# A four-layer macaron kernel on one core: five re-orderings, from the second layer's weight preparation to the first unit of the last attention

## The chip, the core and the metric

The kernel runs on one core of one Trainium2 chip. The metric is the device time of one execution in microseconds (us). The core has a matrix engine (TensorE, PE), a vector engine (VectorE, DVE), a scalar engine (ScalarE, ACT), a general engine (GpSimd, POOL) and a queue engine that issues most DMAs (SyncE, SP). Each works through its own instructions in their program order and waits on semaphores of the others. All data are fp32.

## The reference

Four batches of 512 tokens of width 128 run through four layers. Each layer adds half of a feed-forward block, then an attention (or scan), then half of the same feed-forward block again:

```python
x = x + 0.5 * L0_ffn(layernorm(x)); x = x + L0_attn(layernorm(x)); x = x + 0.5 * L0_ffn(layernorm(x))
x = x + 0.5 * L1_ffn(layernorm(x)); x = x + L1_attn(layernorm(x)); x = x + 0.5 * L1_ffn(layernorm(x))
x = x + 0.5 * L2_ffn(layernorm(x)); x = x + L2_attn(layernorm(x)); x = x + 0.5 * L2_ffn(layernorm(x))
x = x + 0.5 * L3_ffn(layernorm(x)); x = x + L3_attn(layernorm(x)); x = x + 0.5 * L3_ffn(layernorm(x))
```

- L0_ffn: top-1 mixture of 8 experts (128 to 512 to 128, relu) with a capacity of 320 tokens per expert. L3_ffn: top-2 mixture of 8 experts with capacity 512. Tokens beyond an expert's capacity are dropped.
- L1_ffn: sigmoid gate, top 2 of 8 small swiglu experts plus a shared one. L2_ffn: top 2 of 8 linear experts, `gates[e] * ((x @ w_in[e].T) @ w_out[e].T)`, so that each expert is one 128x128 matrix, m = w_out·w_in.
- L0_attn and L1_attn: causal softmax attention with 16 heads of 8 (the former with a table of relative positions, the latter with the product of two low-rank scores). L2_attn: gated decaying scan. L3_attn: full (not causal) softmax attention of 16 heads of 8 over 512 keys, with a layernorm of its own, x + out.

## The kernel before

A batch b is a tile `xs[b]` of 128 partitions by NT = 4 tiles by 128. Feed-forward blocks of layers 1 and 2 are run by pairs of batches, `pairs = [[0, 1], [2, 3]]`. A stage is written as a Python generator; `skewed(gens, lag)` (L1519) advances several of them in turn, the i-th beginning i * lag rounds later, and so writes the order in which each engine's instructions stand. `whole` runs one generator to its end. Outside of `manual_schedule` a planner may move instructions a little; inside, the order written is the order of the queues.

**Mixtures (layers 0 and 3).** `tokens` (L296) normalises a batch's rows (`norms`, L168–L186: BN_STATS and BN_AGGR per tile on DVE, rs and rstd on POOL, then n on ACT or DVE), transposes them (T_f, L195), makes logits (L330), masks (L344 and what follows), the rank of a token within its expert (rank_f, three matmuls at L373 and after) and its target row (`to`, L405–L409), and scatters the rows into a buffer in DRAM, `disp`, with indirect DMAs that POOL issues (L416). The top-2 mixture has two copies of the buffer, one per choice. `experts` (L426) then loads the rows of an expert (d, and d2 for the second copy), and `prepare` (L452) joins them: where a row lies behind the first choice's rows (`behind`, 0 or 1), d2's row is added to d (L457 a multiplication of 128x520, L458 an addition of 128x512, L459 an addition of the two trailing columns). Then four transposes (dT, L463), a copy on ACT (L465), two matmul stages (h_f L487, o_f L523) and a scatter back (L509). `combine` (L533) loads a batch's results (r, L538) and adds them to x (L539). The mixture objects in order are f00 and f01 (layer 0, before and after attention) and f30, f31 (layer 3).

**Layer 2's weights.** `prep_l2` (L1296) loads w_in and w_out of the 8 experts during f01's experts, and then for each expert e transposes w_out (wo2T, L1326), copies it out of PSUM, makes m_e with four matmuls of 2 passes (L1331), and copies that. The copies go through `copy` (L131–L136), which alternates between DVE (L134) and ACT (L136): here all copies of wo2T are DVE's and all of m ACT's.

**Layer 1's first feed-forward block** follows. The main body first runs `f01.combine(b)` for all four batches, then `skewed([followed(pool, bs) for bs in pairs], 12)`; `followed` is `l1_ffn` (L1134: normalise, transpose T_f, logits, routing chain mx L226 to comb L1089, transposed gates gT L1127, expert matmuls), and for pair 0 also the beginning of layer 1's attention.

**Layer 3's dispatch.** At the end of the chain of layers 1 and 2 (`behind` in the main body), the last pair's two batches go through `f30.tokens` with `skewed(..., 3)`.

**Attention 3** is the helper `attention` (L597) without an additive table. A unit u is a batch b and a group g of 4 heads, 16 units in all. For each unit it works in two passes over the scores: `largest` multiplies queries by keys (s_a, L618) and takes each query's negated largest score with DVE (low, L707, 128x512); `lowered` (L709–L716) transposes low and adds it to the queries (ql); `by_key` makes the scores again, keys by (lowered) queries (t_a, L618), whose exponential on ACT (L727) is the weight w, already transposed; `times_values` (L750) multiplies w with the values (L757). `step(f, n)` is one half of one tile (two of the four heads); `together` takes two steps and sets their products in turn. `lead = 10` steps of `largest` are run ahead, with `lowered(0)` after eight (16 reduces); then the loop over u from 0 pairs the largest of 10 steps ahead with the weights of now. Between them stand `start(u + 2)` (q and k of a later unit), `normalized` (L773) and, through `begin_next`, the parts of the next batch's `begin` (L1456: combine's adds, BN, n2 and n, T, qk, values). Each of the four heads lies in its own 32 rows (SLOT) of the array. Products of a query or key tile go to one PSUM bank of 512 columns each; there are 8 banks.

Of the kernel before, what the change touches and what calls it, by code (L numbers as in the profile page):

```python
# [17 lines left out]
P = 128  # L18
# [23 lines left out]
def kernel(ctx: ExitStack, tc: tile.TileContext, a: dict, out: bass.AP):  # L42
# [170 lines left out]
    def bc(ap, shape):  # L213
        while len(ap.shape) < len(shape):
            ap = ap.unsqueeze(len(ap.shape))
        return ap.to_broadcast(shape)
# [28 lines left out]
    class Mixture:  # L245
# [180 lines left out]
        def experts(self, w, beside=None):  # L426
# [3 lines left out]
            with tc.tile_pool(name=f"moe_{self.tag}", bufs=2) as pool:  # L430
# [21 lines left out]
                def prepare(e):  # L452
                    tag = f"{e}_{self.tag}"
                    d = got[e, 0]
                    if self.k == 2:
                        d2 = got[e, 1]
                        nc.vector.tensor_tensor(d2, d2, bc(behind[:, e, :], [P, per, W]), ALU.mult)  # L457
                        nc.vector.tensor_tensor(d[:, :, :D], d[:, :, :D], d2[:, :, 2:], ALU.add)  # L458
                        nc.vector.tensor_tensor(d[:, :, D:], d[:, :, D:], d2[:, :, :2], ALU.add)  # L459
                    ps = bank(f"dT{tag}")  # L460
                    for s in range(per):
                        m = min(P, cap - s * P)
                        nc.tensor.transpose(ps[:, s * P : s * P + m], d[:m, s, :D], ident[:m, :m])  # L463
                    dT = pool.tile([P, cap], FP, name=f"dT{tag}", tag="dT")
                    nc.scalar.copy(dT, ps[:, :cap])  # L465

                    back = pool.tile([P, per], I32, name=f"back{tag}", tag="back", bufs=8)
                    lost = pool.tile([P, per], FP, name=f"lost{tag}", tag="lost", bufs=4)
                    nc.vector.scalar_tensor_tensor(
                        lost, d[:, :, D], 0.0, astray[:, e * per : (e + 1) * per], ALU.is_equal, ALU.mult  # L470
                    )
                    nc.vector.tensor_tensor(back, d[:, :, D], lost, ALU.add)  # L472
                    made[e] = d, dT, back
# [123 lines left out]
    def attention(pool, tag, begin, project, residual, owT, added, after=None, beside=(), fetch=None):  # L597
# [108 lines left out]
                c = r * SLOT + (units[u][1] + 1) % NG * HD  # L706
                nc.vector.tensor_reduce(st["low", u][:, i, c : c + 1], ps, AX.X, ALU.max, negate=True)  # L707

        def lowered(u):  # L709
            q, k = st["qk", u]  # L710
            ps = bank(f"low_{tag}{u}")
            for i in range(NT):
                nc.tensor.transpose(ps[:, i * P : (i + 1) * P], st["low", u][:, i, :], ident)
            ql = pool.tile([P, S], FP, name=f"ql_{tag}{u}", tag="ql", bufs=2)
            nc.vector.tensor_tensor(ql, ps, q, ALU.add)
            st["ql", u] = ql  # L716

        def by_key(u, j, rs):
            q, k = st["qk", u]
            out = []  # L720
            for r in rs:
                ps = bank(f"t_{tag}{u}_{j}{r}")
                yield lambda ps=ps, r=r: product(ps, k, st["ql", u], r * SLOT, j, 0, S)
                out.append((ps, r))
            for ps, r in out:
                w = pool.tile([P, S], FP, name=f"w_{tag}{u}_{j}{r}", tag="w", bufs=8)
                nc.scalar.activation(w, ps, AF.Exp)  # L727
                st["w", u, j, r] = w

        def step(f, n):  # L730

# [5 lines left out]
        def together(*parts):  # L737

            live = [p for p in parts if p is not None]
            while live:  # L740
                for p in list(live):
# [3 lines left out]
                    else:  # L745
                        made()


        def times_values(u, j, half):

            b, g = units[u]
            if j == 0 and half == 0:
                st["acc", u] = bank(f"acc_{tag}{u}")
            acc = st["acc", u]
            n0, n1 = half * S // 2, (half + 1) * S // 2
            for r in range(4):
                nc.tensor.matmul(  # L757
                    acc[r * SLOT : (r + 1) * SLOT, n0:n1],
                    vpads[b % 2][:, j, g * 4 + r, :],
                    st["w", u, j, r][:, n0:n1],  # L760
                    start=(j == 0 and half == 0),
                    stop=(j == NT - 1 and half == 1),
                )
            if j == NT - 1 and half == 1:
                summed(u)
# [49 lines left out]
        with tc.manual_schedule(engines={E_.PE, E_.DVE, E_.Activation, E_.Pool}):  # L815
            while begun(0):
                pass
            for u in range(3):
                if fetch is not None:
                    fetch(*units[u])  # L820
                if u > 0:
                    start(u - 1)
            if added:
                for i in range(NT):
                    scores(0, i)
                    exponentials()
            else:

                for n in range(0, lead, 2):
                    if n == 2 * NT:  # L830
                        lowered(0)
                    together(step(largest, n), step(largest, n + 1))
            for u in range(n_units + 1):
                last = u - 1
                now, nxt = u < n_units, u + 1 < n_units
                for j in range(NT):
                    n = 2 * (u * NT + j)

                    of = (u, j - 1) if j > 0 and now else (last, NT - 1) if j == 0 and last >= 0 else None
                    if added:  # L840
                        if now:
                            weights(u, j)
                        exponentials()

                        if of:
                            values_up_to(*of)
                        if rest or not begin_next(u, True):
                            go_on()
                        if nxt:
                            scores(u + 1, j)  # L850
                    else:
                        together(step(largest, n + lead), step(by_key, n))
                        if of:
                            times_values(*of, 0)
                        if j == NT - 1 and nxt:
                            lowered(u + 1)
                        if rest or not begin_next(u, True):
                            go_on()
                        together(step(largest, n + 1 + lead), step(by_key, n + 1))
                        if of:  # L860
                            times_values(*of, 1)
                    if j == 0 and u + 2 < n_units:
                        start(u + 2)
                    if j == 0 and last >= 1 and units[last - 1][1] == NG - 1:
                        ended(units[last - 1][0])
                    elif not begin_next(u):
                        go_on()
                    if j % 2:
                        next(beside, None)
                    if j == 2 and last >= 0:  # L870
                        normalized(last)
                    if j == 3 and fetch is not None and u + 3 < n_units:
                        fetch(*units[u + 3])
                    if j == 3 and last >= 0 and units[last][1] == NG - 1:
                        gathered(units[last][0])
            ended(NB - 1)
            while rest:
                go_on()
# [417 lines left out]
    def prep_l2(pool):  # L1296
# [22 lines left out]
            nc.gpsimd.tensor_copy(raw[0:1, :, e, 0], behind[0:1, 0:1].to_broadcast([1, 2]))  # L1319
            fetch(e)  # L1320
        yield
        for e in range(E):
            wi, wo = got[e]
            ps = bank(f"wo2T_{e}")
            for c in range(NC):
                nc.tensor.transpose(ps[:, c * P : (c + 1) * P], wo[:, c * P : (c + 1) * P], ident)  # L1326
            woT = pool.tile([P, FF], FP, name=f"wo2T_{e}", tag="woT", bufs=3)
            copy(woT, ps)
            pm = bank(f"m2_{e}")
            for c in range(NC):  # L1330
                nc.tensor.matmul(  # L1331
                    pm[:, :D], wi[:, c, :], woT[:, c * P : (c + 1) * P], start=(c == 0), stop=(c == NC - 1)
                )
            copy(m[:, e, :], pm[:, :D])

    def l2_ffn(pool, i, bs):
        tag = f"f2{i}_{bs[0]}"
# [237 lines left out]
    with tc.tile_pool(name="weights12", bufs=1) as mid:  # L1575
# [7 lines left out]
            whole(made)  # L1583
        first = small.tile([P, 1], FP, name="first_sigmoid", tag="first_sigmoid", bufs=1)
        nc.scalar.activation(first, l2["m"][:, 0, 0:1], AF.Sigmoid)
        for b in range(NB):
            whole(f01.combine(b))
        with tc.tile_pool(name="ahead1", bufs=2) as ahead:
            vpads[:] = [padded(ahead, 0), None]
            begun = l1_begin(ahead)  # L1590

            def followed(pool, bs):
                yield from l1_ffn(pool, 0, bs)
                if bs[0] == 0:

                    yield from begun[0](0)
                    for g in range(2):
                        begun[1](0, g)
                        yield
                        begun[4][0, g] = begun[2](0, g)  # L1600

            with tc.tile_pool(name="ffn10", bufs=2) as pool:
                whole(skewed([followed(pool, bs) for bs in pairs], 12))

            early = []
            with tc.tile_pool(name="gates10", bufs=1) as pool:
# [5 lines left out]
        def behind(pool, bs):  # L1612
# [7 lines left out]
                while next(parts, "end") != "end" and next(parts, "end") != "end":  # L1620
                    yield
            else:
                yield from skewed([f30.tokens([b], l3["gate"], "scalar", pool) for b in bs], 3)

        with tc.tile_pool(name="chain", bufs=2) as pool:
            decay = pool.tile([P, S], FP, name="decay", tag="decay", bufs=1)
# [69 lines left out]
```

## Time and profile before

| | |
|---|---|
| time, median of 3 runs | 1515.85 us (1512.09 to 1516.94) |
| the profiled execution | 1516.03 us |
| its span | 1514.3 us |
| mean granted TensorE clock | 0.914 |
| instructions | 28772 |

The stages as they lie in the trace, in us from the start of the span: f00's experts 62–113, attention 0 113–365, f01's experts 367–420, layer 2's weights and combine 418–443, layer 1's feed-forward block 443–516, attention 1 516–765, the chain of layers 1 and 2 with f30's dispatch 765–1003, f30's experts 1005–1078, attention 3 1081–1413, f31's experts 1427–1497, final addition and output to 1514.

The lines shown further on are of three kinds. A window gives, for a stretch of the span, its length, each engine's busy time with the number of its instructions, the granted TensorE clock (1.00 is full speed), the DMA engines' busy share and GB/s. A line of the timeline gives the start in us, the busy time, engine, source line, operation, output and inputs by the program's names, shape, how many instructions were joined, and in brackets the idle time of the engine before it and who ended it. The chain is the work that ended last, followed back from the end, as shares of the span.

### The profile page before, as it was taken

Reading aid. Unit: us, or ns where it says so; the run is one execution under the profiler, and the core shown is the slowest. Engines: PE = TensorE matmul, PEld = TensorE weight load, DVE = VectorE, ACT = ScalarE, POOL = GpSimd, SP = SyncE. Lnnn points to the kernel's source line nnn. Section 1 sums busy time; section 2 is a strip of 40 time slices with the busy share of each in tenths; the row PEclk is TensorE's granted clock in tenths of the full one; section 3 lists DMA queues with packets and bytes.
Section 4 is the critical chain, followed back from the end, with each engine's and each line's share of the span. In section 5 each row is a group of like instructions: output and inputs, shape, how many; then the busy total and the mean of one; then the engine's idle time right before and its main releaser. Section 6 shows DMA issues by size and latency. Waiting matters only on the chain.

```text
span 1514.3 us, 28772 instructions
## 1 busy us (share of the span) xinstructions
PE 1278.2 (84%) x10645; PEld 817.5 (54%) x10645; DVE 881.6 (58%) x2893; ACT 682.6 (45%) x1431; POOL 696.5 (46%) x808
## 2 busy tenths in 40 slices
PE   4687999995968989998999878739589999998394
PEld 3464666774755656676656656627333434343273
DVE  5336777663356657777566755434287787772343
ACT  1235877871422367776621222104336555563041
POOL 5346767871533578876443112555520323202253
PEclk9898999996989999999999887759799999998597
DMA  8410240002412874241130000032114000000223
GB/s 259 104 53 22 79 171 11 9 7 78 147 36 57 230 241 151 85 142 36 38 76 1 1 0 3 29 90 85 49 42 149 9 12 5 15 1 15 78 82 108
DMA packets 100660, 106.21 MB, mean 70 GB/s; under 512 B 9084, under 2 KB 73832, under 8 KB 100520
## 3 DMA queue, kind: packets, MB, share of 16 engines
q1 hardware_dynamic: 91752, 90.11, 20.7%
q0 software_dynamic: 6656, 13.22, 2.5%
q8 instruction: 84, 1.38, 0.4%
q10 hardware_dynamic: 2112, 1.05, 0.3%
q14 instruction: 56, 0.46, 0.1%
HBM read 62.49 MB, written 41.85 MB: 69 GB/s over the span
## 4 chain that ended last, share of the span: by engine, by line
PE 66%; DVE 9%; POOL 8%; issue 7%; DMA 6%; ACT 2%; SPq 1%; POOLq 0%; ACTq 0%; DVEq 0%
PE s_a L618 13%; PE t_a L663 8%; PE h_f L487 5%; PE acc_a L757 5%; PE o_f L523 5%; PE acc_a L685 5%; PE y_f L1380 4%; PE t_a L618 3%; PE ot_a L776 2%; POOL disp_f L416 2%; POOL res_f L509 2%; PE gate_f L1397 2%; PE lg_f L330 1%; PE T_f L195 1%; DVE low L707 1%
## 5 line engine op out<-in xcount | busy, mean ns | idle before, releaser
L650 POOL TENSOR_SCALAR sc_a<-sc_a,top_a 128x128 f32<-128x128 f32 (+3 forms) x256 | 276.5, 1096 | 84.4 <-DVE top_a L635 58.5
L618 PE MATMUL s_a<-k_a,q_a 32*128 32x512 f32 (+3 forms) x1536 | 262.7, 540 | 5.4 <-DVE top_a L639 3.5
L727 ACT ACTIVATE w_a<-t_a 128x512 f32<-128x512 f32 x256 | 140.2, 595 | 124.2 <-PE t_a L618 92.1
L707 DVE TENSOR_REDUCE low<-s_a 128x1 f32<-128x512 f32 x256 | 163.4, 684 | 47.8 <-PE t_a L618 34.8
L663 PE MATMUL t_a<-ident,sc_a 128*128 128x128 f32 x1280 | 170.9, 279 | 6.1 <-DVE top_a L639 5.3
L618 PE MATMUL t_a<-ql_a,k_a 32*128 32x512 f32 x512 | 169.7, 648 | 0.5 <-DVE low L707 0.2
L509 POOL DMA_INDIRECT res_f<-y_f,back_f x112 | 109.7, 980 | 127.6 <-ACT y_f L508 91.3
L663 PEld LDWEIGHTS t_a<-ident,sc_a 128*128 128x128 f32 x1280 | 142.1, 142 | 41.2 <-issue 15.6
L652 ACT ACTIVATE sc_a<-sc_a,top_a 128x128 f32<-128x128 f32 (+3 forms) x256 | 134.8, 575 | 13.9 <-DVE top_a L639 13.4
L618 PEld LDWEIGHTS s_a<-k_a,q_a 32*128 32x128 f32 x1536 | 92.0, 185 | 77.7 <-issue 42.5
L672 ACT ACTIVATE w_a<-t_a 128x256 f32<-128x256 f32 (+2 forms) x192 | 94.3, 526 | 68.7 <-PE t_a L663 68.2
L416 POOL DMA_INDIRECT disp_f<-n_f,to_f x96 | 95.1, 991 | 55.8 <-issue 37.1
L523 PE MATMUL o_f<-w_l,h_f 128*128 128x128 f32 (+1 forms) x896 | 110.5, 278 | 1.4 <-ACT h_f L491 1.0
L523 PEld LDWEIGHTS o_f<-w_l,h_f 128*128 128x128 f32 (+1 forms) x896 | 102.3, 184 | 10.3 <-DVE back_f L472 4.4
L487 PE MATMUL h_f<-dT_f,w_l 128*128 128x320 f32 (+1 forms) x256 | 104.0, 544 | 2.8 <-ACT dT_f L465 2.8
L685 PE MATMUL acc_a<-w_a,vpad 128*32 128x128 f32 x2560 | 97.6, 278 | 0.6 <-ACT w_a L672 0.6
L674 ACT COPY w_a<-t_a 128x256 f32<-128x256 f32 (+2 forms) x192 | 93.3, 526 | 5.7 <-PE t_a L663 5.3
L172 POOL TENSOR_SCALAR rs_f<-mv_f 128x4 f32<-128x4 f32 (+1 forms) x23 | 5.3, 232 | 194.8 <-DVE mv_f L169 194.3
L639 DVE CUSTOM_DVE_ANT_0 sc_a<-s_a,future 128x128 f32<-128x128 f32 (+3 forms) x128 | 62.3, 487 | 45.0 <-PE s_a L618 41.4
L639 DVE CUSTOM_DVE_ANT_0 sc_a<-s_a,table 128x128 f32<-128x128 f32 (+3 forms) x128 | 62.5, 488 | 44.0 <-PE s_a L618 33.6
L757 PE MATMUL acc_a<-w_a,vpad 128*32 128x256 f32 x1024 | 84.8, 400 | 2.8 <-ACT w_a L727 1.9
L508 ACT ACTIVATE y_f<-o_f,d_f 128x128 f32<-128x128 f32 (+1 forms) x112 | 39.0, 394 | 103.5 <-DVE o_f L503 92.4
(344 smaller groups left out, 2227.3 us busy)
## 6 DMA issues: line engine op xcount, KB each, us to landing
fac_a<-fac_a_sb SPq DMA_DIRECT2D x36, 256.0 KB
disp_f<-zeros_f SPq DMA_DIRECT2D x4, 2080.0 KB
d_f<-disp_f SPq DMA_DIRECT2D x32, 260.0 KB
w_l<-in_L_ffn_w_dram SPq DMA_DIRECT2D x16, 512.0 KB
cb_f<-rows_f SPq DMA_DIRECT2D x16, 512.0 KB
q_a<-fac_a SPq DMA_DIRECT2D x32, 256.0 KB
k_a<-fac_a SPq DMA_DIRECT2D x32, 256.0 KB
r_f<-res_f SPq DMA_DIRECT2D x16, 256.0 KB
```

Source lines behind the costliest of these rows:

```text
L416: nc.gpsimd.indirect_dma_start(out=self.to[c][i0 + t][:, :], out_offset=bass.IndirectOffsetOnAxis(ap=to[:, c, t : t + 1], axis=0), in_=ns[ ...
L487: nc.tensor.matmul(ps[u][:, :cap], w1[:, e, (c + u) * P : (c + u + 1) * P], dT, start=True, stop=True)
L509: nc.gpsimd.indirect_dma_start(out=self.back[e * per + s][:, :], out_offset=bass.IndirectOffsetOnAxis(ap=back[:m, s : s + 1], axis=0), in_ ...
L523: nc.tensor.matmul(po[:m, s, :], h[:, c, s * P : s * P + m], w2[:, e, c, :], start=(c == 0), stop=(c == NC - 1),)
L618: nc.tensor.matmul(ps[:, n0:n1], q[r : r + SLOT, i * P : (i + 1) * P], k[r : r + SLOT, n0:n1], start=True, stop=True)
L650: nc.gpsimd.tensor_scalar(sc, sc, top, None, ALU.subtract)
L652: nc.scalar.activation(sc, sc, AF.Exp, bias=top, scale=-1.0)
L663: nc.tensor.transpose(ps[:, x * n + j * P : x * n + (j + 1) * P], st["sc", u, i, r0 + x][:, j * P : (j + 1) * P], ident,)
L685: nc.tensor.matmul(st["acc", u][r * SLOT : (r + 1) * SLOT, i * P : (i + 1) * P], vpads[b % 2][:, j, g * 4 + r, :], st["w", u, i, r][:, j * ...
L707: nc.vector.tensor_reduce(st["low", u][:, i, c : c + 1], ps, AX.X, ALU.max, negate=True)
L727: nc.scalar.activation(w, ps, AF.Exp)
L757: nc.tensor.matmul(acc[r * SLOT : (r + 1) * SLOT, n0:n1], vpads[b % 2][:, j, g * 4 + r, :], st["w", u, j, r][:, n0:n1], start=(j == 0 and ...
```

## The change

Five edits.

1. In `prepare`, the joining of d2 into d is done slot by slot: per slot one scalar_tensor_tensor of 128x128 (d += d2 * behind), four in all, then a small multiplication and a small addition for the two trailing columns.
2. In `prep_l2`, transposes of expert e stand ahead of m of expert e − 1, and all copies go to ACT.
3. Only pair 0 is combined ahead of layer 1's feed-forward block; pair 1 is combined within `followed`, two rounds ahead of its `l1_ffn`, with a skew of 10 instead of 12, so that `l1_ffn` of pair 1 begins where it did.
4. The last pair's f30 tokens go with a skew of 4 instead of 3.
5. In attention 3 the first unit is written out (`first_unit`): its ql is made in two halves of the queries, its weights in halves of 256 queries (two key tiles to a bank, `by_key_half`), in turn with the largest of units 0, 1 and the start of 2, and the loop over u begins at 1. The next batch's begin parts, which `begin_next` hands out within the loop, so begin in unit 1 instead of unit 0.

```diff
@@ experts.prepare
-                        nc.vector.tensor_tensor(d2, d2, bc(behind[:, e, :], [P, per, W]), ALU.mult)
-                        nc.vector.tensor_tensor(d[:, :, :D], d[:, :, :D], d2[:, :, 2:], ALU.add)
+                        for s in range(per):
+                            nc.vector.scalar_tensor_tensor(
+                                d[:, s, :D], d2[:, s, 2:], behind[:, e, s : s + 1], d[:, s, :D], ALU.mult, ALU.add
+                            )
+                        nc.vector.tensor_tensor(d2[:, :, :2], d2[:, :, :2], bc(behind[:, e, :], [P, per, 2]), ALU.mult)
                         nc.vector.tensor_tensor(d[:, :, D:], d[:, :, D:], d2[:, :, :2], ALU.add)
@@ attention
-        def lowered(u):
+        def lowered(u, n0=0, n1=S):
...
-            for i in range(NT):
+            for i in range(n0 // P, n1 // P):
                 nc.tensor.transpose(ps[:, i * P : (i + 1) * P], st["low", u][:, i, :], ident)
...
+            nc.vector.tensor_tensor(st["ql", u][:, n0:n1], ps[:, n0:n1], q[:, n0:n1], ALU.add)
+        def by_key_half(u, j0, half, rs):
+            q, k = st["qk", u]
+            n = S // 2
+            out = []
+            for r in rs:
+                ps = bank(f"t_{tag}{u}_{j0}{r}{half}")
+                rows = slice(r * SLOT, (r + 1) * SLOT)
+                for x in range(2):
+                    yield lambda ps=ps, rows=rows, x=x: nc.tensor.matmul(
+                        ps[:, x * n : (x + 1) * n], k[rows, (j0 + x) * P : (j0 + x + 1) * P],
+                        st["ql", u][rows, half * n : (half + 1) * n], start=True, stop=True,
+                    )
+                out.append((ps, r))
+            for ps, r in out:
+                w = pool.tile([P, S], FP, name=f"w_{tag}{u}_{j0}{r}{half}", tag="w", bufs=8)
+                nc.scalar.activation(w, ps, AF.Exp)
...
+        def first_unit():
+            top = [step(largest, n) for n in range(lead + 2 * NT)]
...
+            together(top[0], top[1])
+            together(top[2], top[3])
+            products((top[4], 2), (top[5], 2))
+            lowered(0, 0, half)
+            together(top[4], top[5])
+            together(top[6], first[0, 1])
+            together(top[7], first[0, 0])
+            products((top[8], 2), (first[2, 1], 4))
+            products((top[9], 2), (first[2, 0], 4))
+            lowered(0, half, S)
+            together(first[2, 1], first[2, 0], top[8], top[9])
+            for j in range(2):
+                times_values(0, j, 0)
+            together(top[10], other[0, 1])
+            start(2)
+            together(top[11], other[0, 0])
+            for j in range(2, NT):
+                times_values(0, j, 0)
+            together(top[12], other[2, 1])
+            next(beside, None)
+            together(top[13], other[2, 0])
+            together(top[14], top[15])
+            for j in range(2):
+                times_values(0, j, 1)
+            products((top[16], 2), (top[17], 2))
+            lowered(1)
+            together(top[16], top[17])
+            next(beside, None)
...
-                for n in range(0, lead, 2):
-                    if n == 2 * NT:
-                        lowered(0)
-                    together(step(largest, n), step(largest, n + 1))
-            for u in range(n_units + 1):
+                first_unit()
+            for u in range(0 if added else 1, n_units + 1):
...
                         if of:
-                            times_values(*of, 0)
+                            times_values(*((0, NT - 2, 1) if of == (0, NT - 1) else (*of, 0)))
@@ prep_l2
-        for e in range(E):
...
-            copy(woT, ps)
...
-            copy(m[:, e, :], pm[:, :D])
+        for e in range(E + 1):
+            if e < E:
+                ps = bank(f"wo2T_{e}")
...
+                nc.scalar.copy(wT[e], ps)
+            if e > 0:
+                pm = bank(f"m2_{e - 1}")
...
+                nc.scalar.copy(m[:, e - 1, :], pm[:, :D])
@@ main body
-        for b in range(NB):
+        for b in pairs[0]:
             whole(f01.combine(b))
...
             def followed(pool, bs):
+                if bs[0] > 0:
+                    for b in bs:
+                        yield from f01.combine(b)
                 yield from l1_ffn(pool, 0, bs)
...
-                whole(skewed([followed(pool, bs) for bs in pairs], 12))
+                whole(skewed([followed(pool, bs) for bs in pairs], 10))
...
-                yield from skewed([f30.tokens([b], l3["gate"], "scalar", pool) for b in bs], 3)
+                yield from skewed([f30.tokens([b], l3["gate"], "scalar", pool) for b in bs], 4)
```

`products(*parts)` sets a given number of products of each part in turn, without their reductions or exponentials, which `together` adds later.

## The prediction

> **What bounds the kernel now.** I read the page's totals and its chain first, then the windows by stage around each edited place, then the timeline of each place in order of start.
>
> ```profile
> PE 1278.2 (84%) x10645; PEld 817.5 (54%) x10645; DVE 881.6 (58%) x2893; ACT 682.6 (45%) x1431; POOL 696.5 (46%) x808
> ...
> PE 66%; DVE 9%; POOL 8%; issue 7%; DMA 6%; ACT 2%; SPq 1%; POOLq 0%; ACTq 0%; DVEq 0%
> ```
>
> TensorE is busy 84% of the span and carries 66% of the chain. The change removes no TensorE work worth naming, so a gain can only come from the other third: places where TensorE waits. The windows (us, then the busy time of PE, PEld, DVE, ACT and POOL, then granted clock, DMA share, GB/s) show which places those are.
>
> ```profile
> 418.00:443.00 25.00, 13.97 (x109) 12.02 (x108) 14.20 (x52) 6.82 (x18) 7.79 (x12) 1.00 0.17 49
> ...
> 470.00:520.00 50.00, 47.73 (x257) 32.57 (x257) 28.09 (x64) 11.30 (x20) 23.09 (x20) 1.00 0.55 150
> 975.00:1005.00 30.00, 7.92 (x32) 6.54 (x32) 7.18 (x46) 2.73 (x7) 17.86 (x25) 0.51 0.11 36
> 1020.00:1078.00 58.00, 54.25 (x321) 39.76 (x319) 23.10 (x48) 22.41 (x52) 31.34 (x32) 1.00 0.22 67
> 1097.00:1108.00 11.00, 8.19 (x36) 3.58 (x36) 9.66 (x16) 0.25 (x1) 1.42 (x2) 0.87 0.00 0
> ```
>
> 418–443 (m2 preparation), 975–1005 (last dispatch of f30) and 1097–1108 (start of attention 3) leave TensorE room. 470–520 and 1020–1078 are TensorE-bound (47.7 of 50, 54.3 of 58): what comes earlier ahead of them is kept, what is saved on DVE inside them is worth nothing.
>
> **The change part by part.** Each sum is made against the profiled execution, 1516.03 us (span 1514.3), 0.18 above the median of 1515.85. Comparing the two instruction orders, SP's queue keeps its order everywhere; the other queues move only as told here.
>
> *(a) m2 pipelined, and the second pair's combine put off.*
>
> ```profile
> 424.20 0.69 DVE L134 COPY wo2T<-wo2T 128x512 f32<-128x512 f32 x1 [1.69 <-PE wo2T L1326]
> 424.95 1.16 PE L1331 MATMUL m<-wo2T,raw 128*128 128x128 f32 x8 [0.78 <-DVE wo2T L134]
> ...
> 432.39 0.25 POOL L172 TENSOR_SCALAR rs_f<-mv_f 128x8 f32<-128x8 f32 x1 [10.72 <-DVE mv_f L169]
> 434.93 1.65 ACT L182 ACTIVATE n_f<-x,off_f,rstd_f 128x128 f32<-128x128 f32 x4 [2.67 <-POOL off_f L177]
> 441.51 1.13 PE L1331 MATMUL m<-wo2T,raw 128*128 128x128 f32 x8 [2.90 <-issue]
> 442.48 1.44 PE L195 MATMUL T_f<-ident,n_f 128*128 128x128 f32 x8
> ```
>
> Pair 0's rows are normalised at 434.93 + 1.65 = 436.6, yet T_f waits in TensorE's queue to 442.48: the last m product starts at 441.51, because each wo2T copy (0.69) stands in DVE's order among 16 BN_STATS, 16 BN_AGGR and four x adds. After, the copies are ACT's (0.59 + 0.27 per expert; ACT is busy 6.82 of 25), and T of e+1 runs while e is copied. TensorE needs 1.60 per expert (m start 422.57 to the end of the next T, 424.17, in the same timeline): seven from 421.8 end at 433.0, plus 1 to 2 for the n_f activations (1.65) among ACT's copies: m7 ends near 434.5, T_f starts near 435.0, **−7.5**.
>
> Given back later: x adds, BN and n_f of pair 1 now fall into pair 0's routing chain (L226 at 449.34 to comb L1089 at 457.03, gT L1127 at 457.36). On DVE the x3 add and four BN pairs fill gaps and cost +0.5. n_f_2[0] now stands ahead of comb and waits for POOL's rstd_2; behind it on DVE are comb, and behind that TensorE's gT. BN's end to rstd was 2.35 in the trace (432.30 to 434.65), of which 0.52 is covered: +1.83, and +0.34 for n_f itself. That is +2.7, bounds 0 (rstd in time) and +5 (r03's load also late: SP now issues it behind a wait for T_f_0, some 3 us later). POOL's vpad and future memsets, 3.3, move ahead of rs_2; they wait only for m7, so end near 438, before it. Net **−4.8** [−7, −2]; 470–520 keeps it.
>
> *(b) f30 tokens, skew 4.*
>
> ```profile
> 975.89 1.63 PE L195 MATMUL T_f<-ident,n_f 128*128 128x128 f32 x4 [3.04 <-ACT n_f L182]
> 977.31 0.53 PE L373 MATMUL rank_f<-masks_f,not_before 128*128 128x64 f32 x2
> 980.35 0.19 DVE L344 TENSOR_REDUCE mx_f<-lg_f 128x4 f32<-128x32 f32 x1 [1.20 <-PE lg_f L330]
> 982.03 1.12 POOL L416 DMA_INDIRECT disp_f<-n_f,to_f  x1 [6.12 <-DVE masks_f L234]
> ```
>
> Batch 2's rank products stand behind batch 3's T_f, which waits for ACT; and its slot steps (DVE L405–L409, end 981.17) behind batch 3's L344, which waits for logits until 980.35. POOL then issues 16 scatters at 1.26 each, the last at 1001.69, and the first expert's d_f load follows. After, rank goes ahead: masks are there at 975.59, rank ends near 977.2, L409 near 978.4, and POOL starts 0.86 later as before (981.17 to 982.03), at 979.3: −2.77. One POOL copy (L909, 0.31) moves ahead of the last eight scatters: +0.28. Batch 3's own targets (986.75) come before POOL wants them (989.4). **−2.5** [−3, −1].
>
> *(c) prepare split by slot.*
>
> ```profile
> 1008.29 0.70 DVE L457 TENSOR_TENSOR d_f<-d_f,behind_f 128x520 f32<-128x520 f32 x1 [3.07 <-DMA d_f<-disp_f]
> 1009.03 0.69 DVE L458 TENSOR_TENSOR d_f<-d_f,d_f 128x512 f32<-128x512 f32 x1
> 1010.03 1.09 PE L463 MATMUL dT_f<-ident,d_f 128*128 128x128 f32 x4 [23.26 <-DMA d_f<-disp_f]
> ```
>
> The first transpose now waits for one 128x128 step, not two of 128x512. No row has this form; the nearest, tensor_tensor 128x128 of L503, takes 0.28 (bounds 0.17, a small operation, to 0.35, an n_f step): transposes start near 1008.95, −1.08, and as much in f31 (1430.60 to 1429.5). [...] They wait slot by slot, at 0.21–0.28 each. The other 14 preparations lie beside TensorE-bound experts (DVE 23.1 of 58); without that cover each would cost −0.1 (0.28 a step, two small ones of 0.17, for 0.70 + 0.69 + 0.17) to +0.2 (0.35 a step). **−2.1** [−2.4, −0.5].
>
> *(d) attention 3's first unit.*
>
> ```profile
> 1098.12 9.66 DVE L707 TENSOR_REDUCE low<-s_a 128x1 f32<-128x512 f32 x16 [1.19 <-PE s_a L618]
> 1112.10 1.57 ACT L727 ACTIVATE w_a<-t_a 128x512 f32<-128x512 f32 x3 [14.84 <-PE t_a L618]
> 1113.94 1.41 DVE L539 TENSOR_TENSOR x<-x,r_f 128x512 f32<-128x512 f32 x2
> ```
>
> DVE reduces 16 largest scores at 0.604, ql_0 ends 1108.41, ACT has been idle for 14.84. Then ql_1 comes at 1127.30, ql_2 at 1145.13, ql_3 at 1160.16 (a unit without a batch beginning in it: 15.03). Unit 0 also holds batch 1's x adds (1.41), BN (2.1) and more. After, products start once eight reduces are done. To ql_1 DVE does 32 reduces (19.3) and ql (1.0) from 1098.12, plus 5.2 idle in four places where, laid out in program order, reduces wait for TensorE's half products and values (0.6, 1.85, 1.6, 1.15): 1123.6, −3.7. Part is given back, since batch 1's begin lands in units 1 and 2: unit 1 is 15.03 + 1.5 = 16.5 (before 17.83), and qk and v (TensorE 1.88 + 1.16) fall between ql_2 and ql_3: 15.03 + 3.04 = 18.07. ql_3 at 1158.2, **−2.0** [−5, +3].
>
> [...] The half products stream 256 columns from four row groups. In the trace, at 1138.62 to 1138.64, products of different row groups start 0.02 apart, with the next ones of each group 0.5 later: a group doesn't hold the others. [...]
>
> Sum: −4.8 − 2.5 − 2.1 − 2.0 = −11.4; 1516.03 − 11.4 = 1504.6, as a median **1504.5**.
>
> **The rivals.**
> [...]
> - *R2, the routing chain eats the m2 gain*: rstd_2 late by a further 3.3 behind POOL's memsets or r03's landing, gT near 456: (a) = −1.5, 1507.8. Against: 470–520 gets any gT gain whole. [...]
> - *R3, slower*: the granted TensorE clock. It was 0.75 in 443–470 and 0.51 in 975–1005, where TensorE idles, and 1.00 in 470–520. If the new gap between the early T_f (435) and gT (452) lets the clock stay low into 470–520, its 47.73 busy us become 63.6 at 0.75: +15.9. It decides from a mean clock there of about 0.75 down; at 0.73, 1522. Against: the gap grows only from 15 to 17, and TensorE is busier ahead of it.
> - *The skew does nothing*, if another wait holds L409: (b) = 0, 1507, inside the main case's range.
>
> **How the numbers follow.** Main case 0.55 (1504.5; its own range, from the parts' bounds, 1500 to 1508), R1 0.17, R2 0.15, both 0.05, R3 0.08. A measurement of this kernel can tell about 0.3%, 4.5 us, from no change: faster is below 1511.3, slower above 1520.4. Nearly all of the main case and most of R1 and R2 lie below: faster 0.79; both, and the tails of R1 and R2: same 0.13; R3: slower 0.08. The range 1498.5 to 1512 leaves out R3, half of both, and a little below.
>
> **What would show it.** (a) T_f of pair 0 at 435, comb near 452, and the wait ahead of comb named POOL rstd; layer 1's attention starts 4 to 5 earlier. (b) First scatter 2.7 earlier after batch 2's masks. (c) 0.66 from the first step on d_f to the first transpose, for 1.74. (d) Counted from the first reduce: first exp after 7, for 14.0; ql_1 after 25.5, for 29.2; ql_3 after 60.1, for 62.0. The prediction is wrong if the clock differs in 470–520 or 1097–1165, if gT comes no earlier than 456, or if ql_3 comes no earlier after the first reduce.

## The result, and the profile after

The changed kernel takes 1507.37 us (median of 20 runs, 1501.32 to 1513.79), the kernel before 1513.51 in 20 runs beside it: ratio 0.9949, 95% interval [0.9937, 0.9962], which is −7.7 us [−9.5, −5.7]. Forecast were −11.4 and 1504.5. In two later sessions the same kernel came to 0.9942 [0.9922, 0.9963] and 0.9944 [0.9927, 0.9962]. The profiled execution took 1509.34, with a span of 1507.4 for 1514.3.

Two of the windows that were shown of before, now of the kernel after:

```profile
418.00:443.00 25.00, 20.61 (x135) 18.40 (x133) 7.84 (x35) 12.28 (x28) 8.10 (x11) 0.81 0.17 51
...
470.00:520.00 50.00, 48.17 (x260) 32.46 (x260) 30.62 (x80) 13.47 (x24) 21.54 (x20) 1.00 0.58 159
```

TensorE now works 20.6 of the 25 us up to 443, for 14.0 (part of it at half clock: the mean is 0.81 for 1.00); DVE 7.8 for 14.2 (the copies are ACT's). 470–520 is still TensorE-bound at a clock of 1.00, so rival R3 did not come.

The m2 preparation and the routing chain, from the timeline after:

```profile
434.22 2.08 PE L1401 MATMUL m<-wo2T,raw 128*128 128x128 f32 x8 [3.45 <-ACT wo2T L1397]
436.09 1.91 PE L195 MATMUL T_f<-ident,n_f 128*128 128x128 f32 x8
...
453.48 0.35 DVE L186 TENSOR_SCALAR n_f<-x,mv_f,rstd_f 128x128 f32<-128x128 f32 x1 [1.91 <-POOL rstd_f L173]
453.74 0.22 DVE L1156 TENSOR_TENSOR comb_f<-comb_f,total_f 128x64 f32<-128x64 f32 x1
...
454.06 1.87 PE L1194 MATMUL gT_f<-ident,comb_f 128*8 128x128 f32 x8 [6.15 <-issue]
```

T_f starts at 436.09 for 442.48. The last wo2T copy stands among ACT's n_f, so TensorE waits 3.45 for it and then works at half clock (2.08 for what took 1.13). Further on, comb stands behind n_f of pair 1, which waits 1.91 for POOL's rstd: the wait that the prediction named, priced at 1.83.

The dispatch of f30, and the first expert:

```profile
973.60 0.66 PE L373 MATMUL rank_f<-masks_f,not_before 128*128 128x64 f32 x2 [2.91 <-DVE counts_f L391]
...
977.18 1.12 POOL L416 DMA_INDIRECT disp_f<-n_f,to_f  x1 [3.12 <-ACT nT_f L321]
...
978.57 0.19 DVE L344 TENSOR_REDUCE mx_f<-lg_f 128x4 f32<-128x32 f32 x1 [2.25 <-PE lg_f L330]
...
1003.46 1.14 DVE L458 SCALAR_TENSOR_TENSOR d_f<-d_f,behind_f,d_f 128x128 f32<-128x128 f32 x4 [2.95 <-DMA d_f<-disp_f]
...
1004.12 1.09 PE L466 MATMUL dT_f<-ident,d_f 128*128 128x128 f32 x4 [19.18 <-DMA d_f<-disp_f]
```

The first scatter goes 3.58 after rank for 4.72, and ahead of batch 3's L344 instead of behind it. Transposes start 0.66 after the first step on d_f, for 1.74; the four steps take 1.14 together.

Attention 3, DVE's order after:

```profile
1118.28 0.69 DVE L719 TENSOR_TENSOR ql_a<-low_a,q_a 128x512 f32<-128x512 f32 x1 [0.84 <-PE low_a L716]
...
1122.47 1.41 DVE L542 TENSOR_TENSOR x<-x,r_f 128x512 f32<-128x512 f32 x2
...
1136.25 0.69 DVE L719 TENSOR_TENSOR ql_a<-low_a,q_a 128x512 f32<-128x512 f32 x1
...
1154.09 0.69 DVE L719 TENSOR_TENSOR ql_a<-low_a,q_a 128x512 f32<-128x512 f32 x1
```

ql_1 comes 24.9 after the first reduce (1093.34), for 29.2, but ql_2 and ql_3 17.97 and 17.83 later, for 17.83 and 15.03: unit 2 no longer has the 15.0 of a unit without a begin. Batch 1's x adds (1122.47) now stand in unit 1.

### The profile page after: what moved, and what is told of

Its sections match the earlier page's. It is cut to its first block, busy times and chain, and to the rows that moved or that the text cites. A ratio compares the mean times of both kernels' runs of the same rounds, so it can differ in the third digit from the quotient of the medians.

```text
span 1507.4 us, 28892 instructions
## 1 busy us (share of the span) xinstructions
PE 1284.4 (85%) x10677; PEld 828.3 (55%) x10677; DVE 873.8 (58%) x2934; ACT 686.4 (46%) x1439; POOL 691.8 (46%) x808
## 3 DMA queue, kind: packets, MB, share of 16 engines
q10 hardware_dynamic: 2112, 1.05, 0.3%
## 4 chain that ended last, share of the span: by engine, by line
PE 67%; DVE 10%; POOL 7%; issue 6%; DMA 6%; ACT 2%; SPq 1%; POOLq 0%; DVEq 0%; ACTq 0%
PE s_a L621 13%; PE t_a L666 9%; PE h_f L490 5%; PE acc_a L688 5%; PE o_f L526 5%; PE acc_a L826 5%; PE y_f L1451 4%; PE t_a L621 3%; PE ot_a L845 2%; POOL res_f L512 2%; PE gate_f L1468 2%; DMA cb_f<-rows_f 2%; POOL disp_f L416 1%; PE lg_f L330 1%; PE T_f L195 1%
## 5 line engine op out<-in xcount | busy, mean ns | idle before, releaser
L730 ACT ACTIVATE w_a<-t_a 128x512 f32<-128x512 f32 x240 | 131.8, 596 | 108.1 <-PE t_a L621 68.7
L621 PE MATMUL t_a<-ql_a,k_a 32*128 32x512 f32 x480 | 158.8, 644 | 0.4 <-DVE low L710 0.3
L621 PEld LDWEIGHTS s_a<-k_a,q_a 32*128 32x128 f32 x1536 | 93.8, 185 | 73.3 <-issue 38.4
```

The lines of the kernel that those rows point to most:

```text
L621: nc.tensor.matmul(ps[:, n0:n1], q[r : r + SLOT, i * P : (i + 1) * P], k[r : r + SLOT, n0:n1], start=True, stop=True)
```

## The experiments

The theory after comparing the two traces, **P**: the gains stand at the four places about as forecast, except in attention 3, and the difference in the rest is the granted clock, which comes back at another moment in each execution (in attention 3's first unit after 6.8 us at 0.50 in the first trace of before, after 3.4 in the first trace after). The rivals: **S**, that the stretches between belong to the change; that edit 3 or edit 5 is what matters; and for attention 3, **C**, that the first unit lowers the clock by itself.

All kernels were compared by the same marks in their traces, and every ratio of times is to the kernel before on the same chip. The columns of the table give the edits that a kernel has. The marks: T_f, mx and gT are the first of pair 0; the last y is the end of the chain's last product y_f (L1380 of before); the first scatter is that of the last pair; the first T is attention 3's first transpose T_a; ql_1, ql_2 and ql_3 are the starts of the additions that make ql of units 1 to 3. Each column is one execution per trace.

| us between marks | none (before, twice) | 5 | 2 | 3 | 1–4 | 1–5 (three traces) | 1, 2, 4, 5 |
|---|---|---|---|---|---|---|---|
| start to first w_out transpose, same code | 418.8, 421.9 | 422.9 | 422.2 | 423.0 | 419.6 | 419.3, 422.4, 423.0 | 420.9 |
| w_out transpose to T_f | 23.72, 24.62 | 24.34 | 14.88 | 22.08 | 16.27 | 16.75, 16.48, 15.75 | 14.93 |
| T_f to mx | 6.86, 5.02 | 5.03 | 8.47 | 4.57 | 5.41 | 7.32, 5.30, 4.61 | 7.71 |
| mx to gT | 8.02, 6.05 | 6.04 | 7.53 | 7.10 | 8.63 | 10.65, 8.63, 8.62 | 6.90 |
| (a) w_out transpose to attention 1's first score | 101.13, 97.83 | 97.63 | 93.79 | 96.38 | 93.84 | 96.84, 92.74, 91.88 | 91.70 |
| attention 1's first score to the last y, same code | 450.8, 452.5 | 452.2 | 452.8 | 450.3 | 452.4 | 451.7, 450.8, 451.0 | 451.4 |
| (b) last y to first scatter | 11.35, 11.23 | 12.02 | 11.92 | 11.26 | 9.32 | 9.26, 8.68, 8.67 | 9.27 |
| (c) first step on d_f to dT, f30 / f31 | 1.74 / 1.53 | 1.74 / 1.53 | 1.74 / 1.53 | 1.77 / 1.53 | 0.67 / 0.45 | 0.66 / 0.45 | 0.66 / 0.45 |
| attention 3: first T to first reduce | 8.89, 8.90 | 8.75 | 9.31 | 9.15 | 8.80 | 9.27, 8.83, 9.16 | 9.33 |
| first reduce to ql_1 | 29.17, 29.17 | 26.66 | 29.18 | 29.18 | 29.59 | 24.93, 27.61, 25.82 | 24.96 |
| ql_1 to ql_3 | 32.86, 32.87 | 35.83 | 32.87 | 32.86 | 32.87 | 35.81, 35.83, 35.82 | 35.82 |
| (d) first T to ql_3 | 70.93, 70.94 | 71.24 | 71.35 | 71.19 | 71.26 | 70.02, 72.26, 70.80 | 70.12 |

**1. The two kernels once more** (no edit; `after_again`, `before_again`).

> The changed kernel once more, for a second trace of it. Theory P (the gains stand at the five places, and the rest is where in unchanged code the granted clock comes back, which varies from one execution to the next): T_f of pair 0 near 436, gT near 454, first scatter 2.7 after L409's slot step as before, first dT transpose 0.66 after the first step on d_f, ql_1, ql_2, ql_3 at 24.9, 42.9, 60.7 after the first reduce, each within 0.4; but the 1.8 us that the stretch from 520 to 970 gave back, and the 1.1 us between f30's last expert and the first reduce, differ by 1 us or more from the first trace. Theory S (these 2.9 us belong to the change): both stand again within 0.3. Time 1503 to 1510 by both.

> The kernel before once more, for a second trace of it and for what a comparison of a kernel with itself gives. Theory P (in unchanged code one execution differs from another by the granted clock): ratio within 0.25% of 1; from the first w_out transpose to the first score of layer 1's attention 97 to 102 (101.1 in the first trace, 97.6 in the trace with edit 5 alone, which is the same code there); from attention 3's first T to ql_3 70 to 73 (70.9). Theory S (the times between marks belong to the kernel): both within 0.5 of the first trace.

Measured: 0.9942 [0.9922, 0.9963], and 1.0001 [0.9981, 1.0022] for the kernel before against itself. The stretch 520–970 took 450.8 in the second trace after (451.7 in the first) and 450.8 and 452.5 in the two of before; from f30's first transpose to the first reduce the second took 88.0, against 89.2 in the first trace after and 88.1 in the first of before. So theory S falls: what the first trace showed there belongs to that execution. The start, the same code in all, spreads over 4.2 us. (a) spreads over 3.3 within the kernel before (101.13, 97.83); T_f to mx, 6.86 or 5.02, is part of it. Of my numbers, "within 0.4" missed: T_f was at 438.9 and ql_1 at 27.6.

**2. Edit 3 undone** (`no3`).

```diff
-        for b in pairs[0]:
+        for b in range(NB):
             whole(f01.combine(b))
...
-                if bs[0] > 0:
-                    for b in bs:
-                        yield from f01.combine(b)
...
-                whole(skewed([followed(pool, bs) for bs in pairs], 10))
+                whole(skewed([followed(pool, bs) for bs in pairs], 12))
```

> The changed kernel with the combine of all four batches ahead of layer 1's feed-forward block again (edit 3 undone). The two x adds of pair 1 (1.4 us) then stand among pair 0's BN on DVE, and pair 1's BN and n_f ahead of or in the routing chain, but nothing waits for rstd_2 there. Theory P (edit 3 trades 1.4 us ahead of T_f for the 1.9 us wait and 0.7 us of BN behind it, so is worth nothing by itself): T_f near 437.5, gT 453.5 to 455, time within 0.1% of the changed kernel. Rival (the combine put off is what frees T_f): T_f near 440 and gT near 458, 4 us slower.

Measured 0.9924 [0.9900, 0.9948]. From its timeline:

```profile
435.77 1.30 PE L195 MATMUL T_f<-ident,n_f 128*128 128x128 f32 x4 [1.40 <-DVE n_f L186]
...
450.06 0.23 DVE L1156 TENSOR_TENSOR comb_f<-comb_f,total_f 128x64 f32<-128x64 f32 x1
...
450.39 1.86 PE L1194 MATMUL gT_f<-ident,comb_f 128*8 128x128 f32 x8 [3.24 <-issue]
```

No wait stands ahead of comb, and T_f is not later but earlier, 14.9 after the first w_out transpose for 15.8 to 16.8: with pair 1's adds in between, pair 0's n_f come after the last wo2T copy in ACT's order instead of ahead of it. I had that sign wrong. The rival (edit 3 frees T_f) falls.

**3. Edit 2 alone, edit 3 alone** (`only2`, `only3`).

> The kernel before with the pipelined preparation of m2 alone (edit 2). Theory P (edit 2 carries the whole gain of this place, and edit 3 gives back 1 to 3 of it): from the first w_out transpose to T_f 15 to 16 for 23.7 to 24.3, to layer 1's first score 91 to 92 or up to 4 more at a lower clock, time 0.3 to 0.5% faster. Rival (edit 3 is needed): T_f no earlier than 20.

> The kernel before with pair 1's combine put off alone (edit 3). The wo2T copies then stand on DVE without x2, x3 and pair 1's BN among most of them. Theory P: T_f 20 to 22 after the first w_out transpose for 24, but the wait for rstd_2 returns 2 to 3 in the routing chain, so layer 1's first score moves by -1 to +1 and the time by nothing that shows. Rival (edit 3 helps by itself): 2 to 3 us earlier.

Measured 0.9966 [0.9948, 0.9985] and 0.9995 [0.9971, 1.0019]. Edit 2 alone gives T_f at 14.88 and (a) 93.79; five traces with edit 2 and without 3 (`only2`, `no3`, `warm` and `early` twice, the last two kernels below) average 92.9, four with both 93.8 (single traces lie 2 to 5 apart within each group). Edit 3 alone gives T_f 22.08 and its own price in the chain (mx to gT 7.10 for 6.05). So edit 2 carries the gain.

**4. The wait taken out by a later pair 1** (`skew16`).

```diff
-                whole(skewed([followed(pool, bs) for bs in pairs], 10))
+                whole(skewed([followed(pool, bs) for bs in pairs], 16))
```

> The changed kernel with pair 1 six rounds later (skew 16 for 10), which puts comb ahead of pair 1's n_f on DVE and takes the wait for rstd_2 out of the routing chain. Theory P (the 1.9 us wait is on the path): gT near 452, layer 1's attention starts 1.5 to 2.2 us earlier, 0.1% faster. Rival (pair 1's later start costs what the wait cost, since TensorE runs short of work between the pairs): gT near 452, but layer 1's attention no earlier or later, by up to 3 us.

Measured 1.0027 [1.0007, 1.0047], slower: comb comes before pair 1's n_f, mx to gT falls from 10.65 to 8.12 at the same low clock (gT takes 1.86 there, 1.87 in the changed kernel), but attention 1's first score comes 78.6 after gT for 62.1. From its timeline:

```profile
483.35 2.07 PE L1253 MATMUL o_f<-wd1T,h_f 128*128 128x128 f32 x8 [2.64 <-POOL h_f L1265]
485.21 1.49 PE L195 MATMUL T_f<-ident,n_f 128*128 128x128 f32 x6
```

Pair 1's T_f comes only when pair 0's products have run out, TensorE waits for POOL and works in part at half clock (a mean of 0.76 in 470–500, for 1.00 in the changed kernel). The rival is right, and at 16.5 us by far dearer than the 3 I had set.

**5. Edit 5 alone, edit 5 undone** (`only5`, `no5`).

> The kernel before with the first unit of attention 3 written out and nothing else (edit 5 alone). Theory P: ql_3 60.7 after the first reduce for 62.0, so -1.3 at its place, and 1511 to 1514 for the kernel before's 1513.5. Rival (the unit works as forecast but the granted clock comes back later because ACT and TensorE start earlier): ql_3 above 62, no gain or slower.

> The changed kernel with attention 3's first unit as before (edit 5 undone). Theory N (the unit gives 1.3 from the first reduce to ql_3 when the clock is the same, and what the clock does there is as large): from attention 3's first T to ql_3 70.5 to 72.5, time 0 to 0.15% above the changed kernel. Rival G (edit 5 is worth the 0.37% that edit 5 alone showed): 5 us slower than the changed kernel, near 1511.

Measured 0.9963 [0.9947, 0.9979] and 0.9956 [0.9932, 0.9979]. At its place edit 5 gives first T to ql_3 71.24 (70.93 and 70.94 before), and without it the changed kernel has 71.26 (70.02 to 72.26 with it). The two times don't agree with each other: by itself edit 5 gives 5.6 us of which its place shows nothing, within the changed kernel about 0.1%, less than the intervals. The trace of edit 5 alone can't settle it, because the profiled execution was the slowest of its six (1517.90; the others took 1508.38 to 1514.71). What the place shows is how edit 5 loses. Windows from the first reduce on (0–4, 4–12, 12 to ql_1), first of the changed kernel's first trace, then of its second:

```profile
1093.30:1097.30 4.00, 3.96 (x21) 1.35 (x13) 3.96 (x7) 0.00 (x0) 0.95 (x2) 1.00 0.00 0
1097.30:1105.30 8.00, 7.03 (x50) 5.58 (x50) 6.21 (x11) 3.26 (x6) 0.00 (x0) 0.79 0.01 2
1105.30:1118.30 13.00, 13.00 (x122) 7.66 (x120) 10.19 (x18) 6.11 (x11) 0.00 (x0) 1.00 0.01 1
```

```profile
1093.50:1101.50 8.00, 7.09 (x44) 6.38 (x47) 6.06 (x11) 2.23 (x4) 0.00 (x0) 0.68 0.01 2
1101.50:1117.10 15.60, 15.60 (x128) 8.84 (x123) 10.29 (x18) 7.01 (x13) 0.00 (x0) 0.83 0.00 1
```

TensorE waits about 1 us for the first eight reduces (1.01 ahead of 1098.27 in the first trace), and then the clock falls, to a mean of 0.79 or 0.68, just where the first unit has made TensorE the bound; in the second trace it stays low into the third window (0.83), and ql_1 comes 2.7 later. In the kernel before the clock fell at the same place too, but DVE was the bound, and ql_1 was at 29.17 to 29.59 in every trace without edit 5:

```profile
1102.10:1110.10 8.00, 5.19 (x19) 2.07 (x21) 6.37 (x11) 0.00 (x0) 0.00 (x0) 0.69 0.00 0
```

With edit 5 ql_1 follows the time at half clock. Once it has fallen, the clock is 0.50 for 3.4 us in five traces, and ql_1 comes at 24.9 to 25.0 in each (`after`, `no3`, `skew16`, and `early` twice); for 6.8 us in two, with ql_1 at 25.8 (`after_r5`) and 26.7 (`only5`); for 10.2 us in one, with ql_1 at 27.6 (`after_again`).

**6. Filling the gap, and giving DVE its begin parts back** (`warm`, `early`; both on the kernel without edit 3; `warm` adds seven products that nothing reads).

```diff
+                if u == 0 and i == 2:
+                    nc.tensor.matmul(ps[:, : S // 2], ident, k[:, : S // 2], start=True, stop=True)
                 yield lambda ps=ps, r=r: product(ps, q, k, r * SLOT, i, 0, S)
...
             for i in range(n0 // P, n1 // P):
+                for _ in range(2 - i if n1 < S else 0):
+                    nc.tensor.matmul(ps[:, S // 2 :], ident, k[:, : S // 2], start=True, stop=True)
```

> The changed kernel with edit 3 undone, and seven idle products (128x256, all rows, their result overwritten by what comes next in the same bank) set into the first unit of attention 3, where TensorE waits for DVE's reduces: one ahead of each product of the third query tile, three around the first two low transposes. They fill the gap after which the granted clock was 0.50 for 4 to 10 us in five traces with edit 5. Theory C (the first unit loses to the clock that its own gap brings down): clock 1.00 through the unit, ql_1 at 22 to 24 after the first reduce for 25.0 to 27.6, first T to ql_3 66 to 68.5 for 70.0 to 72.3. Rival (the clock falls for another reason, or the four row groups alone don't keep it up): clock 0.50 there again, ql_1 at 25 to 28, the seven products adding up to 1.5.

Measured 0.9944 [0.9924, 0.9964]: no better than the changed kernel. The windows of `warm`, and two lines of its timeline:

```profile
1085.50:1093.50 8.00, 8.00 (x36) 4.42 (x36) 3.49 (x7) 0.98 (x2) 0.00 (x0) 1.00 0.01 2
1093.50:1110.10 16.60, 16.60 (x151) 10.31 (x148) 12.72 (x22) 8.46 (x16) 0.00 (x0) 1.00 0.00 1
```

```profile
1087.26 0.70 PE L707 MATMUL s_a<-k_a,ident 128*128 128x256 f32 x2
1087.89 1.12 PE L621 MATMUL s_a<-k_a,q_a 32*128 32x512 f32 x2
```

The clock stays at 1.00, as theory C expected of it. But ql_1 comes at 28.71: a product over all rows and one over 32 rows take turns (1087.26, 1087.89: 1.68 a pair), which costs more than the clock did. The half that C promised of the time is wrong. From the second ql half on, ql_1 comes after 12.51, as in the changed kernel's first trace.

That the gap brings the clock down is not shown, and one trace speaks against it. Four of the seven products stand ahead of the gap, among the 32-row products that go at the pace of DVE's reduces, so `warm` filled more than the gap. And in `only3`, which has attention 3 as before (first reduce at 1096.44), the clock fell at 1100.60, while TensorE's first wait came at 1104.27:

```profile
1097.20:1100.60 3.40, 3.40 (x15) 1.74 (x12) 3.40 (x6) 0.00 (x0) 0.00 (x0) 1.00 0.00 0
1100.60:1104.20 3.60, 3.60 (x10) 1.46 (x7) 3.60 (x7) 0.00 (x0) 0.00 (x0) 0.50 0.00 0
```

So the stretch of 32-row products at DVE's pace, which all these kernels have, is the likelier cause; no run isolates it.

```diff
+            begun(1)
             lowered(0, half, S)
...
             together(top[11], other[0, 0])
+            begun(1)
```

> The changed kernel with edit 3 undone, and the first two begin parts of batch 1 (its x adds, 1.41, and half of its BN, 0.9) back in the first unit, at the two places where DVE is idle for 1.5 to 1.6 us there. Theory P (in units 1 and 2 what costs 2.96 over the time without edit 5 is the begin, and DVE's part of it holds the reduces): ql_1 unchanged within 0.3, ql_1 to ql_3 33.5 to 34.5 for 35.8. Rival (TensorE's T, qk and v and the copies set those units): ql_1 to ql_3 35.5 to 35.8, no gain.

Measured 0.9916 [0.9891, 0.9942]. DVE's order in `early`:

```profile
1091.78 1.41 DVE L542 TENSOR_TENSOR x<-x,r_f 128x512 f32<-128x512 f32 x2
...
1105.98 0.69 DVE L719 TENSOR_TENSOR ql_a<-low_a,q_a 128x512 f32<-128x512 f32 x1 [0.84 <-PE low_a L716]
...
1125.74 0.69 DVE L719 TENSOR_TENSOR ql_a<-low_a,q_a 128x512 f32<-128x512 f32 x1
1140.76 0.69 DVE L719 TENSOR_TENSOR ql_a<-low_a,q_a 128x512 f32<-128x512 f32 x1
```

The x adds fit into the gap at 1091.78, ql_1 stays at 24.85, and unit 2 has its 15.02 back; unit 1 takes 19.76. ql_1 to ql_3 is 34.79 for 35.82: 1.0 of the 2.96 is DVE's adds and BN in the wrong unit; the other 1.9 remain.

**7. The best of these beside the changed kernel** (`early_r5`, `after_r5`, no new edit).

> The same version once more, beside the changed kernel on one chip: edit 3 undone, two begin parts in the first unit. Theory P (edit 3 costs 1 to 3 us, the two begin parts give 1): 2 to 4 us faster than the changed kernel, ratio to the kernel before 0.991 to 0.9935. Rival (what the marks show is within what the clock does): ratio as the changed kernel's, 0.9945 to 0.9955.

> The changed kernel beside that version: ratio 0.9942 to 0.9955 by both theories, and a third trace of it: from the first w_out transpose to T_f 16.3 to 16.8, gT to mx 8.6 to 8.8 after a clock of 1.00 or 10.5 after one of 0.50, from the first reduce to ql_1 24.9 to 27.6, ql_1 to ql_3 35.8.

Measured 0.9930 [0.9912, 0.9949] and 0.9944 [0.9927, 0.9962] on one chip. First T to ql_3 is 68.96 in this trace and 68.80 in the other, for 70.0 to 72.3; against the three traces whose clock was low for as short a time (70.0 to 70.2) it is 1.2 less, so that gain is shown at its place. That the whole is faster than the changed kernel is likely, not shown: the intervals overlap. `warm` and `early` first ran on a chip where the kernel before took 1498.13 (the stretch of attention 1's first score to the last y took 444 for 451); why isn't known, and only ratios within one chip are used.

## Why the prediction was right, and where a term was off

The direction and the range held, and so did the mechanism at three of the four places; −11.4 was 3.7 too much. The measured ratio on the forecast's base of 1515.85 would be 1508.1, which is where the prediction had R2 (1507.8), not its main case; but R2 did not come. Its chances of 0.17 for R1, the first unit gaining nothing, and of 0.05 for both counted on half products that hold each other's row groups, a term that no run shows: with edit 5 ql_1 came 24.9 to 27.6 after the first reduce for 29.17 to 29.59, and what the runs showed of R1 is batch 1's x adds, which hold unit 1's reduces. Edits 1 and 4 were never run alone; they are shown by their own marks, whose values in traces with the edit lie well apart from those without. Means over traces with and without an edit:

- **(a) forecast −4.8, measured −5.0** (98.9 in three traces without edits 2 and 3, 93.8 in four with both). T_f −7.9 (24.2 to 16.3) for −7.5; the chain's price at equal clock +2.6 (6.05 to 8.63, and 8.02 to 10.65) for +2.7; the wait 1.91 for 1.83. The single traces spread over 3.5 without and 5.0 with, so that the mean meets the forecast to 0.2 is luck. Rival R2 (a further 3.3) did not come. What the prediction did not see is that edit 3 is not needed for any of this.
- **(b) forecast −2.5, measured −2.4**: last y to first scatter 11.56 in five traces, 8.96 in nine; first scatter to the first step on d_f +0.2, POOL's copy.
- **(c) forecast −2.1, measured −2.16**: 1.08 twice, as the timeline of before gave it. Four 128x128 steps took 1.14, 0.29 each, for 0.70 + 0.69 of the two before; their sum did not decide, because transposes wait for one step only (0.66 from the first step to dT).
- **(d) forecast −2.0, measured −0.35** (first T to ql_3 71.13 in five traces without edit 5, 70.78 in six with it). This is the step that failed; single traces with edit 5 lie between 70.0 and 72.3, so even the 0.35 is not clear of zero. ql_1 came at 24.9 to 27.6 for 25.5, mean 25.8: right, but in part by luck, since the sum was made at a clock of 1.00, and ql_1 was at 24.9 to 25.0 with 3.4 us at half clock. What was mis-sized is the return of the begin to units 1 and 2, put at +1.7 (16.5 and 18.07 against 17.83 and 15.03) and measured at +2.96, in every trace (35.82 for 32.86): unit 1 took 17.97 for the 16.5 forecast, unit 2 17.83 for 18.07. Of this, 1.0 is DVE's x adds and half of its BN, by `early`; they hold the reduces in unit 1 as they had in unit 0. Half products that hold each other's row groups did not show: ql_1 came at 24.9 to 25.0 with 3.4 us at half clock, where the sum without them, at a clock of 1.00, gave 25.5, and in the first trace after, half products of two groups and whole ones of the two others start at 1111.29 to 1111.32 and go on side by side. The row of 1138.62 in the prediction shows less than it read there: the kernel sets four products at that place and the trace has eight records (starts 1138.62 to 1138.64 and 1139.15 to 1139.17), so "the next ones of each group" are second records of the same products. The clock, which the prediction watched for in 1097–1165, differed from trace to trace, as told in experiment 5. The first reduce is 0.1 later after the first T in the traces with edit 5, which is within its spread.

The places add up to −5.0 − 2.4 − 2.2 − 0.35 = −9.9. In five traces each, f30's and f31's experts and the wait for attention 3's first T took 0.2, 0.3 and 0.3 more with edit 1 than without (averages, of traces that differ by up to 1.0 among themselves; why wasn't isolated): −9.1, inside the interval of −9.5 to −5.7. The last 1.4, and why edit 5 alone measured 0.37% where its place shows nothing, stay open.

## What to carry to other kernels

A part that is moved out of one unit into the next must be costed as the unit it lands in without it and with it, from two rows that the trace already has (here 15.0 and 17.8), not as its share of one engine's work. When a stage is made TensorE-bound, look at the clock in the stretch ahead of it: the kernel before has 6.8 us at 0.50 there while DVE sets the pace, and with edit 5 such a stretch moves ql_1, from 24.9 with 3.4 us at 0.50 to 27.6 with 10.2. And before believing what one trace gives between marks, take a second trace of the same kernel: here the same code differed by 3 to 4 us, as much as most of the single edits.

## What the hardware showed that was not expected

Among 32-row products at the pace of DVE's reduces the granted clock fell to 0.50: for 3.4 us in `after`, `no3` and `early`, for 6.8 in `before` and `only5`, for 10.2 in `after_again`, and in `only3` with no recorded wait of TensorE ahead of it (busy 3.40 of 3.40 us). With all-row products set among them the clock stayed at 1.00 (`warm`). In the clock records of `before` and `after`, each stretch at 0.50 or 1.00 lasts a whole multiple of 3.41 us (3.41, 6.83, 10.24 and more; the last is ended by the trace), and when it begins changes from one execution to the next: in the changed kernel the fall in the first unit came 5.8 us after the first reduce in one trace (`after`), 7.0 in another (`after_again`). No run shows what brings the clock down.

An all-rows product and a 32-row product went one after the other in `warm` (0.70 and 1.12 in turn, starts 0.63 and 1.05 apart, 1.68 a pair; each all-rows product shares a bank with the 32-row product after it, but not with the one before it), while 32-row products of four groups start 0.02 apart (1138.62 of the kernel before).
